# A second stream of early Fourier transforms in the first half of a selective-scan and spectral-filter kernel

## The chip, the cores and the metric

The kernel runs on one core of a Trainium2 chip. The metric is the device time of one execution in microseconds; times are given as the median of three runs, and the profile is of one further execution. All data are float32.

## The reference, cut to what matters

Two layers follow each other on `x` of shape 4 x 128 x 128 x 128 (batch B, channels C, height H, width W). The first is a selective scan (Mamba) over the L = 16384 pixels of an image, with 256 inner channels and 16 states, then a group norm, a SiLU and the addition of `x`. The second multiplies the spectrum of each image with the spectrum of its filtered self, mixed over four filters.

```python
# layer 0
h1 = relu(xf @ mlp_w1.T + mlp_b1); xm = h1 @ mlp_w2.T + mlp_b2
x_in, z = split(xm @ in_proj_w.T, 2)
u = silu(causal_conv(x_in, conv_w, width 4) + conv_b)
dt, Bm, Cm = split(u @ x_proj_w.T, [8, 24])
delta = softplus(dt @ dt_proj_w.T + dt_proj_b)
h = h * exp(delta * A) + delta * B * u          # for each pixel, channel and state
y = (sum over states of h * C + u * D) * silu(z)
out = y @ out_proj_w.T
x1 = silu(group_norm(out, 4 groups)) + x
# layer 1
a = relu(agg_w @ group_norm([x1, x1], 32 groups) + agg_b)
weights = softmax(a.mean(H, W) @ wg_w.T + wg_b)           # 4 filters
X = rfft2(x1)
product_f = X * rfft2(irfft2(X * filt_f))                 # = X * X * filt_f up to the edge columns
out = irfft2(sum_f weights_f * product_f) + 0.5 * x1
```

## The kernel before, in words

**Block 0** does layer 0 and part of layer 1 in one hand-written software pipeline. The pixels of the four images are cut into 128 chunks of T = 512 pixels: chunk k is the piece i = k mod 32 of batch b = k div 32. A scan instruction works on 128 rows (32 channels times 4 states) and 512 pixels, so a chunk needs 32 scans. It is cut into 16 slots (`NP`); a slot holds two scans. In an even slot these are the places p = 0, 1 of a group of four, in an odd slot the places 2, 3. The program's `todo[slot, phase]` holds what is issued in each slot; within a slot the phases are issued in a fixed order, first `turn`, then `sums`, `pe`, `exps`, `late`, `act`, `pool`, `dbu`, `early`, `gate`, `scans`, `dve`, `end`. This order is kept as written on each engine (`tc.manual_schedule`), so an instruction that waits holds everything behind it on its engine.

For one slot, ScalarE (ACT) computes the decays `da` (L400), GpSimd (POOL) the inputs `hb` = du * B for places 1 to 3 (L370), and VectorE (DVE) the scans (L419). The product of the scan with C is done by GpSimd (L426) or, for places 2 and 3, by VectorE (L421). For place 0, delta * u * B comes by another way: TensorE turns `du` (`du_turn`, L302), ScalarE scales the turned tile with B into `bt` (`bt_act`, L313), and TensorE turns it back into the PSUM bank `b0` (`dbu_turn`, L382, its transposes at L390), from which VectorE's scan reads. `dbu_turn` for slot n is issued in slot n - 1, in phase `turn`; only for even n does it do anything. There is one bank `b0`, so the next turn waits for the scan that read it. The sums over the states are products of TensorE with a selection matrix (`sums`, L440), opened by a product with the diagonal matrix D (L436) where a new half of the channels begins. `gate` (L450) multiplies the finished half with silu(z) on VectorE. PSUM has two banks `pp` for all other products of a chunk, one for `y`, one for `pt` (turned tiles), one for `b0`, and others for `da`.

From chunk 32 on, the group norm of the batch before (`finish`: normalisation, then pooling products `agg`) is woven into the slots. From chunk 52 on, `spectrum` (L475) computes the forward transform of images whose `x1` is already finished and stores it in `spec`, three, three and two images of a group of 8 channels (`CC`) in three consecutive chunks:

```python
return [
    (4, "pe", load), (12, "pe", over_h), (12, "end", evict), (13, "pe", over_w), (13, "end", store),
]
```

`over_h` (L486) transforms along the height into one `pp` bank, ScalarE evicts it (L490), `over_w` (L500) transforms along the width into the next `pp` bank, ScalarE copies that (L504), and SyncE stores it. This is done for the batches below `EARLY` = 2, in 75 chunks, for 25 units.

**Block 1** (L738) does what is left of layer 1, by units: a unit is a group of 8 channels of one batch (64 units, batch 3 later than the others), worked in three blocks of 3, 3 and 2 images. In block t the loop issues `over_h(t)`, `over_w(t-1)`, `products(t-2)`, `back_h(t-7)`, `back_w(t-8)` and `residual(t-9)`. For a unit whose spectrum is in `spec` ("early"), `over_h` does nothing, and `over_w` takes the stored spectrum `sx` in place of TensorE's products `px` (L892); DVE's products are at L902 and L903. The inputs come on SyncE's queue, `xt1` in 6 buffers and `sx` (L829) in 2:

```python
u[n].early = units[n] in s.spectra
if u[n].early:
    u[n].sx = p2.tile([H, CC, 2, WF], F32, tag="sx", name=f"sx_{n}", bufs=2)
    nc.sync.dma_start(out=u[n].sx, in_=s.spec[b][:, c0 : c0 + CC])
```

GpSimd sums the weighted filters `wb` (L850) and the products `y`. TensorE transforms back (`back_h`, `back_w`), VectorE adds the residual (L949), SyncE stores it (L952). During the first units the normalisation of batch 3 and its pooling products are woven in too: `agg_load` (L675) loads a tile of `x1`, `agg_mm` (L679) multiplies it three blocks later, ScalarE sums it. Loads, stores and pooling loads share SyncE's queue, in the order of the program.

Of the kernel before, what the change touches and what calls it, by code (L numbers as in the profile page):

```python
# [26 lines left out]
F32 = mybir.dt.float32  # L27
# [9 lines left out]
SQ = 4  # L37
NP = 16
CC = 8
EARLY = 2  # L40
KEEP = 4
LAG = 7
EPS = 1e-5
# [3 lines left out]
def kernel(ctx: ExitStack, tc: tile.TileContext, a: dict, out: bass.AP):  # L47
# [105 lines left out]
    stats, outs, spectra = {}, {}, set()  # L153
    spec = [dpool.tile([H, C, 2, WF], F32, tag=f"spec_{b}", name=f"spec_{b}") for b in range(EARLY)]
    shared = SimpleNamespace(**{k: v for k, v in locals().items() if k not in ("ctx", "tc")})
    block0(tc, shared)
    block1(tc, shared)


def block0(tc, s):  # L160
    nc, B, NCH, NH, NS, NG, ND, R, NX, KC, HALO, C, L, NF, DI = (
        s.nc, s.B, s.NCH, s.NH, s.NS, s.NG, s.ND, s.R, s.NX, s.KC, s.HALO, s.C, s.L, s.NF, s.DI,
    )
    NT, TH, HP = T // P, T // 2, P // 2
    with ExitStack() as ctx:
        def pool(name, bufs, **kw):
            return ctx.enter_context(tc.tile_pool(name=name, bufs=bufs, **kw))

        p1 = pool("p1", 1)
        p2 = pool("p2", 2)  # L170
# [4 lines left out]
        psp = pool("psp", 2, space=PSUM)  # L175
        psy = pool("psy", 1, space=PSUM)
        pst = pool("pst", 1, space=PSUM)
        psd = pool("psd", 1, space=PSUM)
# [293 lines left out]
                (50, "dve", done),  # L472
            ]

        def spectrum(b, c0, n):  # L475

            g = {}

            def load():
                g["x"] = p1.tile([s.H, 3, s.W], F32, tag="fx", name=f"fx_{b}_{c0}")  # L480
                nc.sync.dma_start(out=g["x"][:, 0:n], in_=s.x1[b][c0 : c0 + n].rearrange("c h w -> h c w"))

            def over_h():
                g["pa"] = psp.tile([s.W, 3, 2 * s.WF], F32, tag="pp", name=f"pp_fa_{b}_{c0}")
                for q in range(n):
                    nc.tensor.matmul(g["pa"][:, q], g["x"][:, q], s.fh, start=True, stop=True)  # L486

            def evict():
                g["sa"] = p1.tile([s.W, 3, 2 * s.WF], F32, tag="fs", name=f"fs_{b}_{c0}")
                nc.scalar.copy(g["sa"][:, 0:n], g["pa"][:, 0:n])  # L490

            def over_w():
                half = s.H // 2
                g["px"] = psp.tile([s.H, 3, 2 * s.WF], F32, tag="pp", name=f"pp_fx_{b}_{c0}")
                for q in range(n):
                    re, im = g["sa"][:, q, 0 : s.WF], g["sa"][:, q, s.WF :]
                    for (data, a, b_), start in (((re, s.fwr, s.fwr), True), ((im, s.fwi, s.fwm), False)):
                        for at, w in ((0, a), (1, b_)):
                            o = g["px"][at * half : (at + 1) * half, q]
                            nc.tensor.matmul(o, data[:, at : at + half], w, start=start, stop=not start)  # L500

            def store():
                x = p1.tile([s.H, 3, 2, s.WF], F32, tag="fq", name=f"fq_{b}_{c0}")
                nc.scalar.copy(x[:, 0:n].rearrange("h c r k -> h c (r k)"), g["px"][:, 0:n])  # L504
                nc.sync.dma_start(out=s.spec[b][:, c0 : c0 + n], in_=x[:, 0:n])

            return [
                (4, "pe", load), (12, "pe", over_h), (12, "end", evict), (13, "pe", over_w), (13, "end", store),
            ]

        n_chunks = B * NCH
        todo = defaultdict(list)
# [19 lines left out]
        for b in range(B - 1):  # L532
            for at, phase, f in finish(s, io, b, NP + 7, norm, agg):
                todo[at + (b + 1) * NCH * NP, phase].append(f)
        chunk = NCH + NCH // 2 + 4
        for b in range(EARLY):
            for c0 in reversed(range(0, C, CC)):
                chunk = max(chunk, (b + 1) * NCH + NCH // 2 + 4)
                if chunk + 3 > n_chunks:
                    break  # L540
                for at, n in ((0, 3), (3, 3), (6, 2)):
                    for slot, phase, f in spectrum(b, c0 + at, n):
                        todo[slot + chunk * NP, phase].append(f)
                    chunk += 1
                s.spectra.add((c0, b))
        for n in range(n_chunks * NP):
            if n % 2 == 0:
                todo[n - 3, "early"].append(partial(exps, n, (0,)))
            todo[n - 1, "exps"].append(partial(exps, n, (1,) if n % 2 == 0 else (0, 1)))
            todo[n - 1, "turn"].append(partial(dbu_turn, n))  # L550
            todo[n, "scans"].append(partial(scans, n))
            if n % 2 == 0:
                todo[n - 2, "dbu"].append(partial(dbu, n // 2))
            else:
                todo[n + 2, "sums"].append(partial(sums, n // 2))
        slots = [n for n, _ in todo]
        with tc.manual_schedule():
            for n in range(min(slots), max(slots) + 1):
                for phase in ("turn", "sums", "pe", "exps", "late", "act", "pool", "dbu", "early", "gate", "scans", "dve", "end"):
                    for f in todo[n, phase]:  # L560
                        f()

# [509 lines left out]
```

## Time and profile before

| | |
|---|---|
| median of 3 runs | 7097.85 us (7094.02 to 7100.94) |
| profiled execution, its time | 7100.83 us |
| its span, from the first to the last instruction | 7099.1 us |
| busy in the span: TensorE, VectorE, ScalarE, GpSimd | 80%, 96%, 87%, 96% |
| mean granted TensorE clock | 0.926 |
| DMA bytes | 1288.54 MB, mean 182 GB/s |
| block 0 / block 1 meet at about | 6340 us of the span |

Engines are named PE (TensorE), PEld (its weight loads), DVE (VectorE), ACT (ScalarE), POOL (GpSimd) and SP (SyncE, which issues nearly all transfers). Times are in microseconds unless a row says ns. Busy shares are means over the whole span and hide that the two blocks have different limits. A row of the timeline has the start, the busy time, the engine, the line, the operation, its output and inputs, and how many instructions run together; in square brackets stands how long the engine stood idle before, and what ended that. A row of waits has who waited for whom, the sum, how often, and the longest.

### The profile page before, as it was taken

To read this page: it belongs to the slowest core of one execution; us is meant where nothing else is said; L and a number is where in the kernel's file an instruction comes from. 1 tells how busy PE (TensorE), PEld (TensorE's weight loads), DVE (VectorE), ACT (ScalarE), POOL (GpSimd) and SP (SyncE) were. 2 spreads that over 40 slices of the span, in tenths; PEclk is the share of its full clock that TensorE was granted. 3 is DMA by queue.
4 is the path that set the end of the run, shared out by engine and by line. 5 is a ranking of instruction groups with operands and counts; after the bars stand their busy time and mean duration, and the time that the engine had idled before them with its cause. 6 is when DMAs were issued, how large, how long until landed. Compare 5 with 4: busy or idle time off the path is not lost.

```text
span 7099.1 us, 95554 instructions
## 1 busy us (share of the span) xinstructions
PE 5656.9 (80%) x28724; PEld 2700.3 (38%) x28724; DVE 6843.7 (96%) x7901; ACT 6144.4 (87%) x13836; POOL 6807.6 (96%) x3010
## 2 busy tenths in 40 slices
PE   6777777787777778787787778887778787877999
PEld 2333333333333333333333333333333333327888
DVE  6999999999999999999999999999999999997877
ACT  6888888888888888888989888898988989878886
POOL 6999999999999999999999999999999999997887
PEclk8988898888989989999999999999999999989999
DMA  6667667667787767777777777777878777768865
GB/s 141 160 153 164 159 149 165 160 150 175 179 196 181 188 169 167 181 181 179 192 193 196 189 174 177 174 184 172 200 188 200 191 170 178 169 143 293 273 218 190
DMA packets 759513, 1288.54 MB, mean 182 GB/s; under 512 B 81728, under 2 KB 192848, under 8 KB 758992
## 3 DMA queue, kind: packets, MB, share of 16 engines
q1 hardware_dynamic: 758848, 1282.16, 72.5%
q8 instruction: 226, 3.70, 0.2%
q14 instruction: 295, 2.42, 0.1%
q10 hardware_dynamic: 144, 0.26, 0.0%
HBM read 1025.52 MB, written 256.58 MB: 181 GB/s over the span
## 4 chain that ended last, share of the span: by engine, by line
ACT 30%; DVE 24%; POOL 18%; PE 10%; issue 10%; DMA 7%; SPq 1%; DVEq 0%; ACTq 0%; POOLq 0%
DVE da L419 12%; ACT da L400 12%; POOL hb L370 10%; POOL hb L426 7%; DVE h L419 7%; ACT L400 3%; DVE hb L421 3%; DMA rdelta<-dd 2%; ACT bt L313 2%; PE px L892 2%; DMA rdu<-dd 2%; ACT L247 2%; ACT L283 1%; ACT delta L283 1%; PE y L440 1%
## 5 line engine op out<-in xcount | busy, mean ns | idle before, releaser
L370 POOL TENSOR_TENSOR hb<-rdu,rB 128x1536 f32<-128x1536 f32 (+2 forms) x1536 | 3612.4, 2370 | 41.6 <-DMA rdelta<-dd 21.2
L400 ACT ACTIVATE da<-rdelta,amat 128x512 f32<-128x512 f32 x4096 | 2792.3, 699 | 123.3 <-DVE h L419 119.3
L426 POOL TENSOR_TENSOR hb<-h,rC 128x1024 f32<-128x1024 f32 (+1 forms) x1048 | 2411.1, 2302 | 89.3 <-DVE h L419 76.6
L419 DVE TENSOR_TENSOR_SCAN da<-da,st,hb 128x512 f32<-128x512 f32 x2000 | 2449.3, 1268 | 38.0 <-ACT da L400 27.1
L421 DVE TENSOR_TENSOR hb<-da,rC 128x512 f32<-128x512 f32 x2064 | 1309.7, 673 | 2.2
L419 DVE TENSOR_TENSOR_SCAN h<-da,st,b 128x512 f32<-128x512 f32 x992 | 1258.7, 1269 | 1.9 <-PE b L390 1.9
L440 PE MATMUL y<-hb,sel 128*32 128x512 f32 x8192 | 1243.4, 681 | 2.9 <-POOL hb L426 2.7
L419 DVE TENSOR_TENSOR_SCAN h<-da,st,hb 128x512 f32<-128x512 f32 x976 | 1223.1, 1255 | 1.4 <-ACT da L400 1.4
L390 PE MATMUL b<-ident,bt 128*128 128x128 f32 x4096 | 723.7, 298 | 448.9 <-DVE h L419 325.2
L239 PE MATMUL pp_cv<-xm,wck 128*128 128x512 f32 x2048 | 1013.7, 640 | 1.5 <-ACT xm L222 0.8
L313 ACT ACTIVATE bt<-pt_dut,xdt 128x256 f32<-128x256 f32 x2048 | 837.6, 473 | 181.1 <-PE pt_dut L302 180.9
L390 PEld LDWEIGHTS b<-ident,bt 128*128 128x128 f32 x4096 | 524.6, 151 | 943.2 <-DVE h L419 650.7
L422 ACT COPY st<-da 128x1 f32<-128x1 f32 x2064 | 267.9, 160 | 441.3 <-DVE hb L421 437.0
L239 PEld LDWEIGHTS pp_cv<-xm,wck 128*128 128x128 f32 x2048 | 396.0, 204 | 651.7 <-issue 420.8
L302 PE MATMUL pt_dut<-ident,du 128*128 128x128 f32 x1024 | 207.8, 337 | 407.2 <-POOL du L319 391.4
L850 POOL TENSOR_TENSOR wb<-wb,term 128x1040 f32<-128x1040 f32 x166 | 398.8, 2403 | 62.0 <-ACT term L840 56.6
L436 PE MATMUL y<-u,diag 128*128 128x512 f32 x512 | 303.3, 676 | 183.7 <-DVE zs L450 181.8
L277 PE MATMUL pp_dt<-xd,wdt 128*128 128x256 f32 x1024 | 299.2, 418 | 149.9 <-ACT pp_o L464 141.2
L302 PEld LDWEIGHTS pt_dut<-ident,du 128*128 128x128 f32 x1024 | 132.2, 165 | 652.6 <-POOL du L319 528.5
L400 ACT ACT_TABLE_LOAD x262 | 336.1, 1283 | 12.2 <-DMA rdelta<-dd 7.6
L319 POOL TENSOR_TENSOR du<-delta,u 128x1024 f32<-128x1024 f32 x128 | 301.1, 2353 | 29.4 <-ACT delta L283 27.9
L228 PE MATMUL pp_z<-xm,win 128*128 128x512 f32 x512 | 275.6, 636 | 59.5 <-ACT fq L504 53.7
(167 smaller groups left out, 8209.6 us busy)
## 6 DMA issues: line engine op xcount, KB each, us to landing
rdelta<-dd SPq DMA_DIRECT2D x1024, 256.0 KB, 4.8
rdu<-dd SPq DMA_DIRECT2D x1024, 256.0 KB, 7.8
rC<-bc SPq DMA_DIRECT2D x512, 256.0 KB, 7.4
rB<-bc SPq DMA_DIRECT2D x512, 192.0 KB, 4.6
dd<-delta SPq DMA_DIRECT2D x256, 256.0 KB, 7.7
dd<-du SPq DMA_DIRECT2D x128, 512.0 KB, 6.6
ft<-in_filt_w SPq DMA_DIRECT2D x108, 520.0 KB, 6.7
ob<-o SPq DMA_DIRECT2D x128, 256.0 KB, 2.1
```

The lines of the kernel that those rows point to most:

```text
L239: nc.tensor.matmul(ps["cv", j], w, d["xm"][:, t : t + T], start=t == 0, stop=t == KC - 1)
L302: nc.tensor.transpose(ps["dut"][:, 2 * t + j, :], d["du"][:, j, at : at + P], s.ident)
L313: nc.scalar.activation(d["bt"][:, 2 * h + t, :, q, :], src, AF.Copy, scale=d["xdt"][:, 2 * h + t, R + q : R + q + 1])
L370: nc.gpsimd.tensor_tensor(hb[:, p : p + n, :], d["du", j][:, m : m + n, :], d["B"][:, p - 1 : p - 1 + n, :], ALU.mult)
L390: nc.tensor.transpose(b[:, t * P : (t + 1) * P], src, s.ident)
L400: nc.scalar.activation(da, d["delta", j][:, m, :], AF.Exp, scale=s.amat[:, c : c + 1])
L419: nc.vector.tensor_tensor_scan(o, das[q], b, init, ALU.mult, ALU.add)
L421: nc.vector.tensor_tensor(hb[:, p + q, :], das[q], d["C"][:, p + q, :], ALU.mult)
L426: nc.gpsimd.tensor_tensor(hb[:, ps, :], h[:, q, :], d["C"][:, ps, :], ALU.mult)
L436: nc.tensor.matmul(y, s.diag[:, j, :], d["u"][:, j, :], start=True, stop=False)
L440: nc.tensor.matmul(y[m * DG : (m + 1) * DG, :], s.sel, d["hb", j, r][:, p, :], start=False, stop=r == NG - 1)
L850: nc.gpsimd.tensor_tensor(wb, wb, u[n].terms[f], ALU.add)
```

## The change

`EARLY` goes from 2 to 3, so images of batch 2 are transformed early too. A second stream of `spectrum` runs beside the first in chunks where both fit. It uses the bank `b0` in place of `pp`: it loads in slot 4, does `over_h` and the eviction at the end of slot 14, and `over_w` and the store at the end of slot 26, that is slot 10 of the next chunk. Both streams now work in place in one tile (`fx` for the first, `fy` in two buffers for the second), where the first had three tiles. The blocks of three, three and two images of a unit go each to the stream that is free first. The turns of `b0` for slots 0 and 12 of a chunk move from phase `turn`, ahead of the sums, to a new phase `late turn` behind them, in all 128 chunks. The first stream has 59 blocks and the second 58 in the chunks 52 to 75, 84 to 107 and 116 to 127; before, the one stream had 75 in chunks 52 to 126. 39 units of block 1 are early in place of 25. Fourteen are new: by number in block 1's order 2, 5, 8, 11, 14, 17, 20 of batch 1 and 28, 31, 34, 37, 44, 51, 58 of batch 2.

```diff
-EARLY = 2
+EARLY = 3
...
-        def spectrum(b, c0, n):
+        def spectrum(b, c0, n, second):
             g = {}
+            tag = f"{b}_{c0}"
+
+            def bank(name, rows):
+                pool, to = (psd, "b0") if second else (psp, "pp")
+                return pool.tile([rows, 3, 2 * s.WF], F32, tag=to, name=f"{to}_{name}_{tag}")
 
             def load():
-                g["x"] = p1.tile([s.H, 3, s.W], F32, tag="fx", name=f"fx_{b}_{c0}")
-                nc.sync.dma_start(out=g["x"][:, 0:n], in_=s.x1[b][c0 : c0 + n].rearrange("c h w -> h c w"))
+                pool, to = (p2, "fy") if second else (p1, "fx")
+                g["f"] = pool.tile([s.H, 3, 2 * s.WF], F32, tag=to, name=f"{to}_{tag}")
+                nc.sync.dma_start(
+                    out=g["f"][:, 0:n, 0 : s.W], in_=s.x1[b][c0 : c0 + n].rearrange("c h w -> h c w")
+                )
...
             def evict():
-                g["sa"] = p1.tile([s.W, 3, 2 * s.WF], F32, tag="fs", name=f"fs_{b}_{c0}")
-                nc.scalar.copy(g["sa"][:, 0:n], g["pa"][:, 0:n])
+                nc.scalar.copy(g["f"][:, 0:n], g["pa"][:, 0:n])
...
             def store():
-                x = p1.tile([s.H, 3, 2, s.WF], F32, tag="fq", name=f"fq_{b}_{c0}")
-                nc.scalar.copy(x[:, 0:n].rearrange("h c r k -> h c (r k)"), g["px"][:, 0:n])
+                nc.scalar.copy(g["f"][:, 0:n], g["px"][:, 0:n])
+                x = g["f"].rearrange("h c (r k) -> h c r k", r=2)
                 nc.sync.dma_start(out=s.spec[b][:, c0 : c0 + n], in_=x[:, 0:n])
 
+            if second:
+                return [
+                    (4, "pe", load), (14, "end", over_h), (14, "end", evict), (26, "end", over_w), (26, "end", store),
+                ]
             return [
                 (4, "pe", load), (12, "pe", over_h), (12, "end", evict), (13, "pe", over_w), (13, "end", store),
             ]
...
-        chunk = NCH + NCH // 2 + 4
+        free = [0, 0]
         for b in range(EARLY):
+            free = [max(c, (b + 1) * NCH + NCH // 2 + 4) for c in free]
             for c0 in reversed(range(0, C, CC)):
-                chunk = max(chunk, (b + 1) * NCH + NCH // 2 + 4)
-                if chunk + 3 > n_chunks:
+                steps, now = [], list(free)
+                for at, n in ((0, 3), (3, 3), (6, 2)):
+                    q = now.index(min(now))
+                    steps += [(slot + now[q] * NP, phase, f) for slot, phase, f in spectrum(b, c0 + at, n, q == 1)]
+                    now[q] += 1
+                if max(slot for slot, _, _ in steps) >= n_chunks * NP:
                     break
-                for at, n in ((0, 3), (3, 3), (6, 2)):
-                    for slot, phase, f in spectrum(b, c0 + at, n):
-                        todo[slot + chunk * NP, phase].append(f)
-                    chunk += 1
+                free = now
+                for slot, phase, f in steps:
+                    todo[slot, phase].append(f)
                 s.spectra.add((c0, b))
...
-            todo[n - 1, "turn"].append(partial(dbu_turn, n))
+            todo[n - 1, "turn" if n % NP not in (0, 12) else "late turn"].append(partial(dbu_turn, n))
...
-                for phase in ("turn", "sums", "pe", "exps", "late", "act", "pool", "dbu", "early", "gate", "scans", "dve", "end"):
+                for phase in ("turn", "sums", "late turn", "pe", "exps", "late", "act", "pool", "dbu", "early", "gate", "scans", "dve", "end"):
```

## The prediction

> **What bounds the kernel now.** I read the busy time by stage first. The stretches are: block 0 without finishing work, with pooling products and early transforms, with normalisation; then block 1 early, in the middle and late. Columns: length, busy us of PE, weight loads, DVE, ACT, POOL, granted clock, DMA share, GB/s.
>
> ```profile
> 300.00:1500.00 1200.00, 941.13 (x3899) 383.37 (x3897) 1199.59 (x1244) 1028.06 (x2302) 1186.66 (x518) 0.89 0.67 157
> 2630.00:3220.00 590.00, 477.41 (x2291) 205.56 (x2290) 586.89 (x611) 525.67 (x1206) 580.94 (x254) 0.97 0.75 177
> 3400.00:4000.00 600.00, 472.51 (x2238) 207.88 (x2236) 596.73 (x646) 538.60 (x1222) 595.27 (x260) 0.92 0.80 194
> 6450.00:6610.00 160.00, 146.99 (x1511) 135.31 (x1510) 155.41 (x331) 138.56 (x275) 136.41 (x70) 1.00 0.92 322
> 6675.00:6770.00 95.00, 90.54 (x714) 72.87 (x712) 71.22 (x164) 85.27 (x193) 82.12 (x42) 1.00 0.79 263
> 6850.00:7075.00 225.00, 218.44 (x2290) 202.65 (x2288) 178.78 (x401) 170.90 (x360) 193.06 (x97) 1.00 0.61 212
> ```
>
> Block 0 is DVE's: under 4 us idle in 590. A chunk takes 48.4 us (even) or 49.1 (odd), so each wait of DVE there is lost time, while PE and ACT have 13 to 20% to spare. Early transforms already run in 2630 to 3220 beside a full DVE. Block 1 has three owners: DVE to 6610 (97%), PE in the middle (95%, POOL 86%, ACT 90%), PE late (97%). A unit moved out of block 1 pays only where PE owns it.
>
> Next the clock, at the hole that PE has in a chunk between the next chunk's `h1` products and the gate product. Two chunks without and with a fall of the clock, cut at the clock's own steps of 3.41 us:
>
> ```profile
> 2901.58:2904.99 3.41, 1.70 (x6) 0.72 (x6) 3.41 (x4) 3.41 (x10) 3.41 (x3) 1.00 0.89 226
> 2904.99:2908.41 3.42, 3.42 (x19) 1.62 (x19) 3.42 (x5) 3.01 (x9) 3.42 (x3) 1.00 1.05 211
> ...
> 2751.39:2754.81 3.42, 1.29 (x6) 0.42 (x4) 3.42 (x5) 3.42 (x11) 3.42 (x2) 1.00 0.82 290
> 2754.81:2758.22 3.41, 2.56 (x6) 0.70 (x10) 3.41 (x5) 3.19 (x8) 3.41 (x3) 0.50 1.07 220
> ```
>
> PE busy 1.70 of 3.41 us keeps the clock; 1.29 halves it for the next step. Over all steps of block 0 the border is at about 1.5 us (44%): nearly all below fall, hardly any above 1.7. The timeline of the second chunk shows what a fall costs:
>
> ```profile
> 2753.90 0.66 PE L390 MATMUL b<-ident,bt 128*128 128x128 f32 x4 [1.88 <-DVE h L419]
> ...
> 2755.66 2.08 PE L436 MATMUL y<-u,diag 128*128 128x512 f32 x2 [1.10 <-DVE zs L450]
> ...
> 2757.66 1.94 PE L440 MATMUL y<-hb,sel 128*32 128x512 f32 x8
> ...
> 2759.53 1.12 PE L302 MATMUL pt_dut<-ident,du 128*128 128x128 f32 x4
> ...
> 2760.68 0.47 ACT L313 ACTIVATE bt<-pt_dut,xdt 128x256 f32<-128x256 f32 x1 [2.69 <-PE pt_dut L302]
> ...
> 2762.63 2.47 DVE L419 TENSOR_TENSOR_SCAN da<-da,st,hb 128x512 f32<-128x512 f32 x2 [1.11 <-POOL hb L370]
> ```
>
> The turn of `b0` for slot 12 (L390) sits in the hole. At half clock the sums take 1.94 instead of 1.07, the turn of `du` ends 2.3 us later than in the chunk at 2900, ACT stands 2.69 us before `bt` with its decays behind it, and DVE waits 1.11 (the row names POOL, but ACT's last decay ended 0.1 before). An odd chunk, which has one DVE product more, lost 0.39.
>
> Last, SyncE's waits from 6660 to 6790:
>
> ```profile
> SPq L952 <- DVE sq L902: 46.9, 12, 10.4
> ...
> SPq L829 <- DVE sq L903: 23.5, 8, 5.7
> ```
>
> Already now the load of `sx` (2 buffers) stops the whole load queue until DVE has read an older unit.
>
> **The change, part by part.** *(1) Fourteen units leave block 1's forward work.* By the order of units these are 2, 5, 8, 11, 14, 17, 20 (batch 1), 28, 31, 34, 37, 44, 51, 58 (batch 2). A full unit has 24 matmul passes of `pa` and 96 of `px`: 0.76+1.48 us for three images, 0.54+1.04 for two (PE timeline, 6902 to 6910), so 6.0 us of PE; ACT gives back about 1 us (three copies of `sa`, 0.44 each, overlapping). Late, units 39 to 63: three more early units, at most 18 us. POOL, 193 of 225 us busy, becomes next. Two units' outputs that straddle an existing early unit there are 18.9 us apart, beside 23.4 without: 4.5 of 6.0 are realised. Three times 4.5, less 1.5 because POOL is near: -12. Unit 20: -3. Units 34 and 37, after the pooling products: POOL's 9.4 us a unit (three sums of 2.40, two thirds of the units, else two; 2.98 for `y`) against 10.3 now, two units: -2. The seven up to 17 lie under DVE at 97%: 0; the 0.53 MB that each reads extra raise a DMA share of 0.92 by 5%; the traffic peaks above 400 GB/s in slices, so I take 0 (bound +5).
>
> *(2) The load queue, units 28 to 34.* From unit 26 on every unit is early, and in the built order the load of `sx` for unit 28 stands ahead of the pooling loads L675. Its buffer is unit 26's, free after DVE's L902 at block 80, three blocks after the place where the load stands; so it goes on for each unit. A pooling load is issued three blocks ahead of its product. That lead is now gone: `sx` issues 0.02 us after L902, L675 0.42 later and lands 4.3 on (SyncE's timeline at 6705): 4.7 us in which PE holds the product and what is queued behind it, `back_h` and `back_w`, and ACT the pooling sum. Before, this was covered by three blocks of some 3.4 us. Round trip for a unit: 4.7, product 1.0, back steps 2.15, product 1.0, `back_h` of two images 0.95, DVE's eviction, residual and L902 with waits 1.6: 11.4 us. That is at full clock. PE then stands 2 to 3 us in each 11, more than the 1.9 that let it fall in block 0; wholly at half clock the 5.1 of PE double: 16.5. I take 13.0, nearer to the first since the back steps keep two thirds of the steps busy. Now a unit takes 10.7 there: 7 x 2.3 = +16. Bounds: -8 (the load is hidden and POOL sets 9.5) to +40.
>
> *(3) `b0`'s turns of slots 0 and 12 go behind the sums, in all 128 chunks.* Slot 0's turn waits now for DVE's scan 14 and ACT's last `bt`; the sums in front of it (1.07) end before these: 0. Slot 12's turn leaves the hole (0.66 us) and stands before the turn of `du`. At full clock this ends 0.66 later, and there is slack: the fall above delayed it 2.3 and cost 1.1, so 1.2 was free. At half clock it adds 1.1, and scan 12 waits too: 2.2 for an even chunk, 1.6 for an odd. The chunk at 2900 keeps 1.70-0.66 = 1.04 in its step and would fall. Done for the 69 chunks without second stream, at their present steps: five fall newly (about 1.2 each, part of the step only), three that fall already (2560, 2608, 5731) pay 1.3 more each: +10.
>
> *(4) The second stream's products, 58 blocks.* Weights pass half as long: 12 `over_w` groups take 1.56 us (L500), `over_h` 0.9 (L486), ACT's two copies 0.48 each. `over_w` fills the same hole, starting when scan 10 frees the bank (1.3 us after it starts, 1.8 before the gate). Queued behind it on PE: the gate product, unaffected when it starts on time. ACT's copy stands after `h1`, ending 5.1 us after scan 10's start, the sums 5.2: the turn ends at 5.9, scan 12 starts at 6.5; `du`'s turn 6.5, free until 6.9. So 0 at full clock; with this slack gone, up to 0.5 x 58 = +29. In slot 14 `over_h`, copy, sums and turn end 1.4 us ahead of scan 16: 0. SyncE's store waits where it waits for the first stream's store now (9.7 us each): 0. ACT's 1 us more per chunk falls before idle times of 1.0 and 1.5 us in slots 17 and 18. Falls of the clock: DVE loses 9.3 us in these chunks now; with 1.56 in the hole instead of 0.66, but late in it, the steps that hold the 1.9 us before it come to 1.5 us, the border itself, and a two-image block (1.05) stays under it. About a dozen falls, each dearer by (3): 14. Difference +5.
>
> *A rule against rows.* The steps with 1.29 us of work fell. The Trainium skill (TensorE: Matmul & The Clock Gate, Part 1) has half clock follow an idle window of about 3.4 us, and elsewhere allows idle gaps up to that; no hole here is wholly idle so long, so by it (3) and (4) would be 0 and the sum 15 us lower. The trace decides for the rows.
>
> Sum: -12 -3 -2 +16 +10 +5 = +14. The profiled execution was 7100.83 us, 2.98 over the median: 7115 for it, **7112 us** beside the median, slower by 0.2%, about what a measurement can tell from no change. Taken by blocks: block 0 +15, block 1 -1.
>
> **Rivals.** *Faster.* The queue's stop in (2) is covered, because the sums of `wb` make POOL the owner (9.5 a unit) and products land before PE wants them: then (2) is -8, and if the streams keep the hole's clock (3)+(4) is +3: about -22, 7076. It decides from a landing under 2.7 us after the issue. For: L675's shortest landing is 2.6. Against: the median behind an `sx` load is 4.3. *Slower by more.* Half clock holds through (2), 16.5 a unit: +40, sum +38, 7136. For: PE waits in every round. Against: a busy step in between restores it. *No change*: (2) at 11.4 gives +5, sum +3, 7101. That the change does not do what it says is out: the built order has 39 loads of `sx` in place of 25.
>
> **Numbers.** Forecast 0.44, slower rival 0.21, no change 0.12, faster 0.23. The forecast lies on the border of 0.2%, so its chance is split, 0.26 slower and 0.18 within: slower 0.47, same 0.30, faster 0.23. Eight in ten: from the faster case's own 7076 to 7145, the slower rival with another third of (4)'s bound; the forecast's own range is 7106 to 7124.
>
> **What would show it.** Right: units 28 to 34 more than 11.4 us apart with PE waiting for the DMA of L675, clock under 1.00 there; units after 39 shorter by about 12 in all; DVE idle in block 0 up, before scans 12 and 13, most in chunks near 2560, 4110 and 5730. Wrong: those units at 9.5, or DVE waits on `b0` in all chunks with two streams.

## The result and the profile after

The changed kernel takes 7097.67 us (12 runs, 7090.3 to 7102.97), beside 7097.62 for the kernel before in the same 12 rounds: ratio 0.9999, 95% interval 0.999 to 1.0008. The change moves the time by nothing that can be measured. The forecast, 7112, is 14 us above it, on the border of "slower" and outside that interval, which ends some 6 us above the kernel before; the range, 7076 to 7145, holds the time.

Nothing on balance does not mean that nothing happened. Cut at VectorE's last scan, the profiled executions give (us, spans 7099.1 and 7096.7; a unit is taken to end with the last residual of its third block):

| stretch | before | after | difference | forecast |
|---|---|---|---|---|
| start to first scan | 50.5 | 48.9 | -1.6 | 0 |
| block 0, first chunk | 67.4 | 68.3 | +0.9 | 0 |
| block 0, chunks 1 to 127 | 6267.2 | 6273.9 | +6.7 | +15 |
| last scan to end of unit 0 | 59.4 | 54.7 | -4.7 | 0 |
| units 1 to 20 | 213.0 | 211.4 | -1.6 | -3 |
| units 21 to 25 | 52.5 | 53.1 | +0.6 | (2): +16 |
| units 26 to 31 | 63.5 | 78.9 | +15.4 | with the line above |
| units 32 to 38 | 72.7 | 69.2 | -3.5 | -2 |
| units 39 to 63 and the end | 252.8 | 238.2 | -14.6 | -12 |

The first line is no effect of the change: it lies between 47 and 52 us in the runs below, whatever the kernel. Block 0 differs a little between executions of one program too: from the first scan to the last, the changed block 0 took 6342.3 us here and 6347.5, 6341.5 and 6342.1 in three runs below that alter block 1 alone; the block 0 before took 6334.7, and 6334.3 in a second execution. So block 0 did become longer, by some 7 to 13 us, and differences of a few us between single executions of it mean nothing.

The same stage windows as before, of the changed kernel (length, busy us of PE, weight loads, DVE, ACT, POOL, granted clock, DMA share, GB/s):

```profile
2630.00:3220.00 590.00, 493.10 (x2594) 224.57 (x2587) 588.21 (x613) 534.32 (x1230) 581.18 (x255) 0.98 0.78 185
3400.00:4000.00 600.00, 482.38 (x2391) 218.20 (x2388) 595.88 (x646) 538.70 (x1227) 595.17 (x261) 0.92 0.80 196
6450.00:6610.00 160.00, 124.12 (x1113) 113.14 (x1114) 155.04 (x331) 132.19 (x261) 136.78 (x70) 0.98 0.95 338
6675.00:6770.00 95.00, 74.68 (x466) 58.88 (x465) 60.04 (x139) 71.39 (x158) 71.36 (x37) 0.93 0.68 231
6850.00:7075.00 225.00, 215.14 (x2210) 199.75 (x2209) 188.32 (x426) 174.78 (x370) 203.15 (x102) 1.00 0.68 237
```

The first two lines are block 0: TensorE has 16 and 10 us more to do, and VectorE is as full as before. In the third, TensorE lost 23 us of work and VectorE still has 155 of 160: early units gain nothing there. The fourth is the stop that step (2) forecast: no engine is busy over 80% of it, the granted clock is 0.93. In the fifth, GpSimd has gone from 193 to 203 us: the units are shorter and it is close behind TensorE.

The stop, in the waits of the changed kernel from 6690 to 6790 (line shifts: pooling load L692, product L696, its sum L700, load of `sx` L846) and in SyncE's rows from 6706 on:

```profile
DVE sz L953 <- PE pz L948: 31.1, 12, 4.2
ACT pf_agg L700 <- PE pf_agg L696: 25.2, 15, 3.3
POOL wb L867 <- ACT term L857: 20.8, 12, 2.5
PE pf_agg L696 <- DMA x<-x: 17.5, 8, 3.3
```

```profile
6710.11 0.86 SPq L842 DMA_DIRECT2D xt<-x  x1
6720.52 0.32 SPq L846 DMA_DIRECT2D sx<-spec  x1
6720.93 0.38 SPq L692 DMA_DIRECT2D x<-x  x1
```

```profile
SPq L846 <- DVE sq L920: 109.0, 14, 11.8
```

The last line is SyncE's wait from 6640 to 6850. SyncE issues nothing from 6710.97 to 6720.52, because the load of `sx` waits for its buffer; the pooling load behind it goes out 0.41 us later, lands at 6725.82 by the trace, and TensorE stands before the product of it: 17.5 us in 8 waits, 2.2 each, as the prediction had it (2 to 3). ACT and VectorE wait for TensorE in turn.

In block 0, the scans of VectorE from 2500 to 6300, before and then after (busy, mean ns, idle before and its releasers); the second form is the scan of place 0, which reads `b0`:

```profile
L419 DVE TENSOR_TENSOR_SCAN da<-da,st,hb 128x512 f32<-128x512 f32 x1202 | 1472.7, 1269 | 31.2 <-ACT da L400 21.2 <-POOL hb L370 8.1 <-issue 1.2
...
L419 DVE TENSOR_TENSOR_SCAN h<-da,st,b 128x512 f32<-128x512 f32 x598 | 759.1, 1269 | 1.9 <-PE b L390 1.9
```

```profile
L419 DVE TENSOR_TENSOR_SCAN da<-da,st,hb 128x512 f32<-128x512 f32 x1200 | 1471.2, 1270 | 17.8 <-ACT da L400 17.3 <-POOL hb L370 0.2
...
L419 DVE TENSOR_TENSOR_SCAN h<-da,st,b 128x512 f32<-128x512 f32 x597 | 759.0, 1271 | 21.7 <-PE b L390 21.5
```

The wait has changed its place: VectorE stood before the scans of places 2 and 3, which wait for late decays; now it stands before the scan of place 0, which waits for the turn of `b0`. Here and below the scans of a chunk are numbered 0 to 31: scans 24 and 25 are those of slot 12, scans 26 and 27 those of slot 13. (The prediction numbers them by slot: its scan 12 is scan 24 here.) By chunks, without the first, the waits before scan 26 went from 11.3 us to none, those before scan 24 from none to 22.3 us in 21 chunks.

### The profile page after: what moved, and what is told of

Same layout as the page of the kernel before. It is cut to its first block, busy times and chain, and to the rows that moved or that the text cites. A ratio compares the mean times of both kernels' runs of the same rounds, so it can differ in the third digit from the quotient of the medians.

```text
span 7096.7 us, 95901 instructions
## 1 busy us (share of the span) xinstructions
PE 5629.8 (79%) x28724; PEld 2706.5 (38%) x28724; DVE 6841.6 (96%) x7901; ACT 6149.4 (87%) x13878; POOL 6810.7 (96%) x3010
## 5 line engine op out<-in xcount | busy, mean ns | idle before, releaser
L370 POOL TENSOR_TENSOR hb<-rdu,rB 128x1536 f32<-128x1536 f32 (+2 forms) x1536 | 3614.2, 2371 | 48.9 <-DMA rdelta<-dd 20.8
L239 PE MATMUL pp_cv<-xm,wck 128*128 128x512 f32 x2048 | 991.5, 629 | 73.1 <-ACT zs L233 72.2
L390 PE MATMUL b<-ident,bt 128*128 128x128 f32 x4096 | 714.7, 299 | 178.5 <-DVE h L419 123.3
L390 PEld LDWEIGHTS b<-ident,bt 128*128 128x128 f32 x4096 | 513.1, 151 | 713.8 <-DVE h L419 400.1
L436 PE MATMUL y<-u,diag 128*128 128x512 f32 x512 | 300.7, 670 | 235.4 <-DVE zs L450 234.4
L440 PEld LDWEIGHTS y<-hb,sel 128*32 128x32 f32 x8192 | 175.7, 112 | 512.3 <-issue 273.2
L400 ACT ACT_TABLE_LOAD x262 | 336.1, 1283 | 12.1 <-DMA rdelta<-dd 7.4
```

What stands on the lines that cost most here:

```text
L239: nc.tensor.matmul(ps["cv", j], w, d["xm"][:, t : t + T], start=t == 0, stop=t == KC - 1)
L370: nc.gpsimd.tensor_tensor(hb[:, p : p + n, :], d["du", j][:, m : m + n, :], d["B"][:, p - 1 : p - 1 + n, :], ALU.mult)
L390: nc.tensor.transpose(b[:, t * P : (t + 1) * P], src, s.ident)
L400: nc.scalar.activation(da, d["delta", j][:, m, :], AF.Exp, scale=s.amat[:, c : c + 1])
L440: nc.tensor.matmul(y[m * DG : (m + 1) * DG, :], s.sel, d["hb", j, r][:, p, :], start=False, stop=r == NG - 1)
```

## The experiments

Each is compared with the kernel before in its own rounds; block 0 is from the first to the last scan in the profiled execution (6334.7 before, 6342.3 after).

**The late turn alone.** The kernel before, without second stream:

```diff
-            todo[n - 1, "turn"].append(partial(dbu_turn, n))
+            todo[n - 1, "turn" if n % NP not in (0, 12) else "late turn"].append(partial(dbu_turn, n))
```

> The kernel before with only the turns of b0 for slots 0 and 12 moved behind the sums; no second stream. Theory A (the place of the turn is what block 0 pays): block 0, 6334.7 us from the first scan to the last in the kernel before and 6342.3 in the changed one, becomes 5 to 8 us longer; DVE's waits before scan 26 of a chunk (11.3 us before) go to nearly 0 and waits before scan 24 for PE's L390 of 15 to 22 us come in their place; whole time +5 to +8 us. Rival B (the second stream's own copies and products are what block 0 pays): block 0 within 1.5 us of before, no waits before scan 24.

Measured: 7137.36 us, ratio 1.0058 (1.0046 to 1.0071); block 0 6372.6, +37.9, block 1 as before. The kind is theory A's (45.0 us of waits before scan 24, 3.0 left before scan 26); the size is far above it, where 5 to 8 us were expected. The scans of the same window, and the chunk that fell in the kernel before near 2851, here at its clock steps and in its timeline:

```profile
L419 DVE TENSOR_TENSOR_SCAN h<-da,st,b 128x512 f32<-128x512 f32 x593 | 753.2, 1270 | 37.6 <-PE b L390 37.5
```

```profile
2857.24:2860.66 3.42, 0.46 (x2) 0.00 (x0) 3.42 (x5) 3.42 (x10) 3.42 (x3) 1.00 0.89 289
2860.66:2864.07 3.41, 2.73 (x6) 0.71 (x10) 3.41 (x5) 3.04 (x8) 3.41 (x2) 0.50 1.07 217
```

```profile
2861.34 2.07 PE L436 MATMUL y<-u,diag 128*128 128x512 f32 x2 [3.64 <-DVE zs L450]
2863.34 1.94 PE L440 MATMUL y<-hb,sel 128*32 128x512 f32 x8
2865.21 1.12 PE L390 MATMUL b<-ident,bt 128*128 128x128 f32 x4
...
2866.36 1.28 DVE L419 TENSOR_TENSOR_SCAN h<-da,st,b 128x512 f32<-128x512 f32 x1 [1.52 <-PE b L390]
```

With the turn gone from the hole, TensorE is busy 0.46 of 3.42 us, the next step runs at half clock, and now the turn stands behind the slow sums, 3.9 us later than the gate's product (L436) starts. Of the waits, 35 are in the 60 chunks where the changed kernel has its two streams, and 28.8 of the 37.9 us in the 36 of them that also carry pooling products.

**Products in the hole, and nothing else of the second stream.** The kernel with the late turn alone, and in each chunk from 50 on, where the second stream would have its `over_w`:

```diff
+        def fill(k):
+            px = psd.tile([P, 3, 2 * s.WF], F32, tag="b0", name=f"fill_{k}")
+            for q in range(3):
+                for w in (s.fwr, s.fwi):
+                    for at in range(2):
+                        o = px[at * HP : (at + 1) * HP, q]
+                        nc.tensor.matmul(o, s.ident[:, at * HP : (at + 1) * HP], w, start=w is s.fwr, stop=w is s.fwi)
...
+            todo[10 + k * NP, "end"].append(partial(fill, k))
```

> The kernel with the late turn alone (no second stream, block 0 6372.6 us, 35 waits before scan 24 in the chunks that would have two streams), with 12 products of 128 x 64 by 128 x 130 on constants put into b0's bank at the end of slot 10 of each chunk from 50 on, where the second stream has its over_w; nothing reads them, so no copy, no eviction and no transfer is added. Theory F (the second stream's products fill TensorE's hole and keep its clock, and that makes the late turn cheap): block 0 falls back by 20 to 35 us to 6338 to 6352, with at most 12 waits before scan 24 in those chunks and fewer half-clock stretches at the hole. Rival G (it is something else of the second stream, its loads or copies, or the changed places of other work): 6365 us or more.

Measured: 7093.84 us, ratio 0.9997 (0.9989 to 1.0006); block 0 6329.4, 43.2 less than without the products, and 9 us below the range given for theory F. The same window and the same chunk:

```profile
L419 DVE TENSOR_TENSOR_SCAN h<-da,st,b 128x512 f32<-128x512 f32 x599 | 760.1, 1269 | 6.4 <-PE b L390 6.4
```

```profile
2848.77:2852.18 3.41, 1.53 (x6) 0.46 (x6) 3.41 (x5) 3.41 (x11) 3.41 (x3) 1.00 1.02 326
2852.18:2855.60 3.42, 3.22 (x34) 1.62 (x32) 3.42 (x4) 3.42 (x8) 3.42 (x3) 1.00 0.96 226
```

Work that nobody needs makes block 0 shorter by 43 us: the hole no longer costs the clock, and the turn behind the sums comes in time. Counted over the 60 chunks, a step at half clock falls on the gate's product (0.3 to 2.0 us after scan 22 starts) in 33 with the late turn alone and in 2 with the fill; it was 19 in the kernel before and is 9 in the changed one. The mean granted clock of the run is 0.943, 0.933 without the fill; but the mean is no measure of the time, for it is 0.926 in the kernel before, which is as fast: it matters where the falls lie. In the changed kernel the second stream's products do the same in this chunk, 3.21 us busy in the corresponding step:

```profile
2849.79:2853.20 3.41, 1.54 (x8) 0.47 (x8) 3.41 (x5) 3.41 (x11) 3.41 (x3) 1.00 0.98 334
2853.20:2856.61 3.41, 3.21 (x34) 1.55 (x30) 3.41 (x4) 3.41 (x8) 3.41 (x3) 1.00 1.03 238
```

**The same products in the kernel before**, all turns ahead of the sums (edit as above, without the late turn):

> The kernel before with the same 12 products on constants at the end of slot 10 of each chunk from 50 on, all turns ahead of the sums as they were. Theory F: the steps at the hole keep the clock, so the waits before scan 26 (11.3 us in 19 chunks) shrink to under 5; but the turn of slot 12 stands right behind the fill: block 0 between -6 and +3 us against 6334.7. Rival G (what holds the clock at the hole plays no part): waits before scan 26 as before or more, block 0 unchanged or, if the fill itself delays the turn of du, 10 us or more longer.

Measured: 7095.32 us, ratio 1.0001 (0.9992 to 1.001); block 0 6333.3, -1.3. The chunks with pooling products from 50 on are 13.1 us shorter than before; the others from 64 on are 10.7 longer, 8.8 of it in the five chunks 65, 81, 96, 97 and 113 at the two ends of a normalisation (the cause is not shown; chunks 65 and 97 come back below). From chunk 50 on the waits before scan 26 went from 10.9 to 7.5 us, not under 5. So in the kernel before the fill is worth nothing on the whole: it gains in the chunks with pooling products, where the hole costs the clock, and loses about as much in the others.

**The second stream without the late turn.** The changed kernel with every turn back in phase `turn`:

```diff
-            todo[n - 1, "turn" if n % NP not in (0, 12) else "late turn"].append(partial(dbu_turn, n))
+            todo[n - 1, "turn"].append(partial(dbu_turn, n))
```

> The changed kernel with all turns back in the phase ahead of the sums; second stream kept. Theory A: waits before scan 24 in chunks without a second stream vanish (9.7 us in the changed kernel), waits before scan 26 return to about those of before (11 us); where the second stream is in the bank, the turn now holds the sums until ACT has copied the bank, the turn of du comes 1 to 2 us late and scan 26 waits in many of the 58 chunks: block 0 between +5 and +60 us against the changed kernel. Rival B: the place does not matter, block 0 within 2 us of the changed kernel.

Measured: 7174.74 us, ratio 1.0114 (1.0098 to 1.0129); block 0 6411.8, 69.6 above the changed kernel, more than the 60 allowed. VectorE waits before scan 26 in 56 of the 60 chunks with two streams, 74.7 us together. The late turn is what makes the second stream bearable: a turn ahead of the sums holds them until ACT has emptied the bank (from 2540 to 6200, TensorE stands 212.9 us before the turn, L390, for ACT's copy of `over_w`, L512).

**Late turn only where the second stream was in the bank.**

```diff
+                    if f.__name__ in ("over_h", "over_w") and phase == "end":
+                        late.add(slot)
...
-            todo[n - 1, "turn" if n % NP not in (0, 12) else "late turn"].append(partial(dbu_turn, n))
+            todo[n - 1, "late turn" if n - 2 in late else "turn"].append(partial(dbu_turn, n))
```

> The changed kernel with a turn behind the sums only where the second stream has just been in the bank; all other turns ahead of the sums as before. Theory A: the waits before scan 24 in chunks 33, 49 to 52, 78 to 84 and 114 to 116 (10 us in the changed kernel) go, some waits before scan 26 return: block 0 3 to 6 us shorter than the changed kernel's 6342.3. Rival B: no change of block 0.

Measured: 7086.54 us, ratio 0.9989 (0.998 to 0.9998); block 0 6330.2, 12.1 less than the changed kernel, where 3 to 6 were expected; the run with both repairs below, with the same block 0, has 6331.0. In the chunks from 50 on without second stream the waits before scan 24 (8.5 us) are gone and 2.1 before scan 26 are there.

**Block 0 of the changed kernel with block 1 of the one before.**

```diff
-                u[n].early = units[n] in s.spectra
+                u[n].early = units[n] in s.spectra and (b == 0 or (b == 1 and c0 >= 56))
```

> Block 0 as in the changed kernel, with 39 early units stored; block 1 uses only the 25 early units of the kernel before, the other 14 are transformed again. Theory A+C (block 0 costs 7 to 8 us and block 1 gives 8 back, as the sum of a 16 us stop and 24 us of gains): +7 to +8 us against before, block 1 from the last scan 714 us as before, no stop at units 26 to 31. Rival D (block 1 gives nothing, both blocks are as before and the differences are of the run): within 2 us of before.

Measured: 7103.74 us, ratio 1.0012 (1.0003 to 1.0021), +8.7; block 0 6342.1, units 26 to 31 63.5, units 39 to 63 249.1 (without the end), both as before. Block 0's cost is real, and block 1 gives it back.

**The load of `sx` three blocks later**, in the changed kernel:

```diff
-                if u[n].early:
+        def load_sx(n):
+            if 0 <= n < N and u[n].early:
+                c0, b = units[n]
...
                     load(n + 2)
+                    load_sx(n + 1)
```

> The changed kernel with the load of sx issued three blocks later, with the loads of the unit after it, so that its buffer is free or nearly so where it stands in SyncE's queue. Theory C (the stop of the load queue costs units 25 to 31 15.9 us): these units take again about 116 us in place of 131.9, waits of SyncE for L919 fall from tens of us to under 10, the pooling product no longer stands before its DMA; 10 to 16 us faster than the changed kernel. Rival E (in that stretch POOL or the DMA traffic of the extra 0.53 MB a unit sets the pace): within 3 us of the changed kernel.

Measured: 7074.7 us, ratio 0.9963 (0.995 to 0.9977), 23 us faster than the changed kernel, more than the 16 expected. SyncE still waits for the buffer of `sx`, 33.2 us from 6640 to 6850 beside 109.0, where under 10 were expected; but no pooling product waits for its load any more. Units 21 to 25 take 50.5 us and 26 to 31 57.2: the 2.6 and 21.7 us less go below the kernel before too (52.5 and 63.5), since the gain of the early units there had been under the stop. The window of 6675 to 6770 in this run, whose unit 25 ends 2.1 us after the changed kernel's:

```profile
6675.00:6770.00 95.00, 85.11 (x606) 67.60 (x605) 79.16 (x178) 89.72 (x206) 89.24 (x47) 1.00 0.88 296
```

DMA moves 296 GB/s in place of 231 and GpSimd and ACT are 94% busy: it was not the traffic that held these units (rival E falls).

**Three buffers of `sx`** (`bufs=2` to `bufs=3`), order unchanged:

> The changed kernel with three buffers of sx in place of two; order of loads unchanged. Theory C: as with the later load, 10 to 16 us faster than the changed kernel, since the buffer that a load waits for is then one unit older. Rival E: within 3 us.

Measured: 7074.56 us, ratio 0.9967 (0.9954 to 0.9979); units 21 to 31 take the same 50.5 and 57.2 us. Two different edits that let the load go in time give one result: the buffer is the cause.

**The later load in the kernel before.**

> The kernel before with the load of sx three blocks later. Theory C: the waits of SyncE for sx there (46.9 and 23.5 us from 6660 to 6790) were covered by the three blocks of lead, so 0 to 3 us faster than before. Rival E': the old waits cost as well, 5 us or more faster than before, and the gain of the later load in the changed kernel is not the price of the change.

Measured: 7096.74 us, ratio 0.9999 (0.999 to 1.0007); no stretch of block 1 moved by over 1.6 us. SyncE's waits in the kernel before cost nothing.

**Both repairs together**, late turn where used and later load:

> The changed kernel with the late turn only where the second stream was in the bank, and the load of sx three blocks later. Theories A and C together: the sum of the two, 13 to 22 us faster than the changed kernel and than the kernel before, 7076 to 7085. Rivals: 7092 or more.

Measured: 7064.84 us, ratio 0.9952 (0.9939 to 0.9964): faster than both kernels, 33 us where 13 to 22 were expected, and close to the sum of the two repairs as measured (11 and 23). With the turn of slot 12 done twice from chunk 50 on:

> The version with the late turn only where the second stream was in the bank and the load of sx three blocks later (7064.84), with the turn of slot 12 done twice from chunk 50 on, which adds 0.6 us of TensorE work in the hole. Theory F: where the turn is in the hole the clock falls less often, 0 to 3 us faster; where it is behind the sums it delays the turn of du by 0.6, up to 58 chunks times 0.6 = 35 us slower if there is no slack there. Rival G: only the delay, slower by 5 us or more.

Measured: 7061.17 us, ratio 0.9953 (0.9939 to 0.9966). The two can't be told apart by their ratios. Block 0 is 6328.0 beside 6331.0; the waits before scan 24 and 26 are 10.5 us beside 12.2. The 3 us between the blocks are no more than two executions of one block 0 can differ by, so a gain is not shown. That the doubled turn does no harm where it delays the turn of `du` says that there is slack while the clock is kept.

## Why the prediction was right or wrong

**Block 1, step (2), was right in mechanism and size.** The sum gave 16 us for the stop of the load queue; units 21 to 31 are 16.0 us longer, and the two repairs show that it is the stop. That the sums agree so closely is partly luck: six units take 2.6 us more each, and units 21 to 25 0.6 together, where the sum had seven units at 2.3. Units end 13.1 us apart in it (78.9 by 6) where 13.0 was taken; the pooling load shown landed 4.9 us after its issue where the sum had 4.3; the granted clock was 0.93, so the choice nearer to full clock than to half held. The stop shows in the outputs of units 26 to 31 and not, as the prediction's sign had it, of 28 to 34 (of these only 29 to 31 are more than 11.4 apart): a unit's residual comes nine blocks after its transform, so the loads of `sx` for units 28 to 34 are issued (6695.23 to 6772.39) while units 24 to 30 are put out. The faster rival's bound for the case without a stop, -8, is what the repaired kernels show: 107.7 us in place of 116.0.

One reading there was wrong. Of the two waits of SyncE shown, that at L952 is the store of `out`, not the load of `sx`, and it is still there when the stop is repaired (85.5 us from 6640 to 6850 with the later load). Only L829 was the load.

**Step (1) was a little small.** Late units gave 14.6 where the sum had 12, units 32 to 38 3.5 for 2, units 1 to 20 1.6 for 3. The sum missed the start of block 1: from the last scan to the end of unit 0 the six kernels with 25 early units take 56.5 to 59.5 us, the seven with 39 take 54.7 to 56.3, 2.7 less in the mean; why is not shown. The bound of +5 for the extra traffic was not needed.

**Step (3) was sized too high.** It put +10 on the late turns of the chunks without a second stream; these chunks became longer by 3.8 us in the profiled execution. Three further executions of the same block 0 (the runs with the later load, with three buffers and with the old block 1) have 9.0, 5.0 and 3.7, so the term is not far off, and its size changes with the execution. The step added the wait of scan 24 to that of scan 26, 2.2 us for an even chunk and 1.6 for an odd. The runs show that most of the one takes the place of the other, since everything behind scan 24 has moved with it: the chunk shown of the late turn alone, an even one, waits 1.52 before scan 24 and then 0.34 before scan 26, where it waited 1.11 before scan 26 in the kernel before, so it pays 0.75 more and not 1.1; in that whole run the waits before scan 24 are 45 us and those before scan 26 3. What the term had right is that the hole without the turn falls below the border: 8 chunks from 50 on without second stream wait before scan 24, near 2560 and 5730 as the prediction named them, and from 4150 on where it said 4110. Its sign that VectorE would also wait longer before slot 13 (scan 26) did not come.

**Step (4) had about the right sum, +2.9 for +5, from the wrong parts.** It took a dozen falls, and 11 chunks wait. But nine of these waits are 6.8 us, less than the 8.4 for which VectorE stood before scan 26 in these chunks before (the prediction's sum has 9.3 for it), and the products in the hole keep the clock: without them the late turn costs 37.9 us, with them and nothing else -5.3 against before. The step weighed the two streams' products only as work that comes late in the hole; the runs with and without the fill show that they pay for the late turn. The other two waits were not foreseen, in the chunks where the group norm's variance is formed:

```profile
3293.66 1.27 ACT L209 ACTIVATE h<-pp_h,mlp_b 128x512 f32<-128x512 f32 x2
...
3294.40 0.38 PE L617 MATMUL pp_gv<-q,g 128*128 128x1 f32 x2 [2.02 <-ACT h L209]
...
3296.31 0.48 ACT L512 COPY fy<-b_fx 128x390 f32<-128x390 f32 x1 [1.38 <-PE b_fx L509]
...
3298.94 1.28 DVE L419 TENSOR_TENSOR_SCAN h<-da,st,b 128x512 f32<-128x512 f32 x1 [2.56 <-PE b L390]
```

The variance product needs a `pp` bank that `h1` still holds, TensorE stands 2.02 us, and the second stream's `over_w`, queued behind it, starts at 3294.7 (by the trace), late enough to push the gate's product, the sums and the turn: 2.56 us here and 3.23 in the chunk at 4887. This is read from the timeline; no run tests it alone, but the fill, queued in the same place, has waits of 2.0 us in the same two chunks. The step said that the gate's product would not be delayed when the stream starts on time; here it doesn't start on time.

**The rule against the rows.** By an idle window as the condition, (3) and (4) would have been nothing, block 0 unchanged. (That no hole is wholly idle holds for the holes that these steps touch; another one, near slot 7, is idle for a whole step 14 times in block 0 of the kernel before, after the first chunk.) In the late turn alone no step shown is wholly idle (0.46 of 3.42 us busy), the clock still falls and block 0 is 37.9 us longer; with the fill, a step with 1.53 of 3.41 us keeps it. The rows decided rightly, though the border is not sharp: with the fill, 24 of the 64 full-speed steps with 1.5 to 1.7 us are followed by half clock. What block 0 paid in the changed kernel lay between the two only because the stream fills most of the holes.

**As a whole**, the forecast had the sign of every term that it named; it was 8 us off in block 0 and 7 in block 1, both to the slow side, and of the 8 some 5 are within what executions of one block 0 differ by. The rival "no change" was nearest in time; it expected 11.4 us a unit in the stop, and that was not why.

## What to carry to other kernels

When an instruction is moved behind a wait, ask whether the old wait stays: on a chain through one engine a new wait can take the place of most of the old one behind it (here 45 us came and 8 of 11 went), and only the difference is to be counted. A hole in TensorE's work that is near the border of its clock can be worth filling, even with work that nobody reads, but only where its successors are on the path: 43 us in one kernel here, nothing in the other. And a load that stands in a shared queue ahead of its free buffer stops all loads behind it (here 24 us over 11 units): give it one more buffer or its place three blocks later, before counting the gain of more such loads.

## What the runs showed of the hardware

The clock goes by the busy share of its steps of 3.41 us. In the trace of the kernel before, from 60 to 6380 us, 179 of the 181 full-speed steps with TensorE busy under 1.5 us are followed by a step at half clock, 11 of the 55 with 1.5 to 1.7, and 2 of the 1325 with more.

A chunk's wait for the clock moves all later chunks against these steps. Undisturbed even and odd chunks of 48.37 and 49.11 us advance by 0.17 and 0.39 of a step, so a kernel meets the steps in another pattern after each fall: of the 12 chunks from 52 to 63, VectorE waits before scan 24 or 26 in 4 in the kernel before, in 10 with the late turn alone, in 2 in the changed kernel. Whether one given chunk falls can't be told from its own work alone. The four executions of the changed block 0 show it: of their even chunks from 4 to 30, the ten whose scan 22 starts 3.05 to 3.26 us after the beginning of a step wait 0.87 to 0.89 before scan 24, and none of the other 46 does. Those ten are chunks 14, 20 and 26 in two executions and 10, 16, 22 and 28 in a third; the fourth has none.
